# Second pair's keys and Gram matrices among the first pair's work, layernorm and evacuations on ScalarE, last products one iteration later

## The chip, the cores and the metric

The kernel runs on one core of a Trainium2 chip. A core has five engines with a queue each: TensorE (PE, matrix products; its loading of weights, PEld, overlaps them), VectorE (DVE), ScalarE (ACT), GpSimd (POOL) and SyncE (SP), which here only issues DMAs. Matrix products end in PSUM, from where DVE or ACT carries ("evacuates") them to SBUF; GpSimd doesn't touch PSUM in this kernel. Each engine runs its instructions in order and waits for the others by semaphores.

The metric is the device time of one execution in microseconds (us), as the median of several. The profile comes from one execution and has a span, from its first to its last instruction, that is a little shorter.

## What is computed

The input x has 32 sequences of 512 rows and 256 features, all in float32. A "delta rule" attention block, an MLP and a gated MLP follow, each with a layernorm ahead of it:

```python
def delta(x, ...):                       # per sequence: T = 512, C = 256
    qkv = x @ gates_w + gates_b
    q, k, v = jnp.split(qkv, 3, axis=-1)
    lr = x @ lr_w + lr_b
    k = k / jnp.linalg.norm(k, axis=-1, keepdims=True)
    K = jnp.tril(jnp.einsum('ntc,nsc->nts', k, k), k=-1)
    A = K + jnp.eye(T, dtype=x.dtype)
    u = jax.scipy.linalg.solve_triangular(A, v, lower=True)
    score = jnp.einsum('nsk,ntk->nst', q, k)
    y = jnp.einsum('nst,ntv->nsv', score, lr * u)
    return y @ out_w + out_b

x0 = x
x = norm(x);  x = x + delta(layernorm(x, dn_g, dn_b), ...)
x = x + relu(layernorm(x, mn_g, mn_b) @ w1 + b1) @ w2 + b2
x = x0 + x
h = silu(norm(x) @ wg.T) * (norm(x) @ wu.T)      # 768 hidden; int32 weights / 127
out = x + h @ wd.T
```

## The kernel before

**Tiling.** A sequence is four tiles of 128 rows (`NT`) by two halves of 128 features (`NF`). The hidden layer of the gated MLP has six tiles (`NH`). Sequences are worked on in 16 pairs (`NS` = 2). Weights of the attention block are folded into each other at the start (`Gates`, L166 to L285), so that a pair needs only keys, a Gram matrix, a triangular solve and a chain of small products.

**A pair's stages.**

1. `normalized` (L405): statistics, centring on ACT (L426), scaling on DVE (L441), two one-column copies on GpSimd; then `Turn` (L374): DVE transposes 32x32 blocks, SP writes them to DRAM and reads them back with features on the partitions (`ag`). The first pair's are transposed on PE instead (`to_features`, L365). `rates` (L460) follows. `prepare` (L850) interleaves both sequences.
2. `keys` (L476): two products of 512 columns; ACT copies `kT` and `aT`. `gram` (L491): four products of 512 to 128 columns; ACT copies the diagonal block `gd`, DVE the rest `go`. `give` (L511) sends the 32x32 diagonal blocks to DRAM.
3. `norms` (L523): the keys' norms, eight reductions on DVE and a power on GpSimd. `invert` (L543): reads the blocks of both sequences, one block's eight columns to a partition, and inverts them in 31 rows on DVE, a product (L568) and a reduction (L572) each; SP writes the result to `found` and reads it back as `yb` and into `yfull`.
4. `merge` (L595) and `solve` (L653): the blocks of 32 become blocks of 64 and 128, then the four row tiles are solved in turn (`pr`, `rhs`, `pu`, `p`, `dp`). `solution` (L861) steps both sequences.
5. `values_phase` (L939): `gather`, `through_values`, `through_keys`, `answer`: the products of the attention's output; then the layernorm for the MLP (`normed`: `Norm.measure` and `Norm.apply`, both on DVE, and a `Turn`).
6. `residual` (L767): `b2s` and `a` are added to a second load of x (`xb`), which is the running sum from then on; `mlp_in`, `mlp_out`, and a further layernorm and `Turn`.
7. Gated MLP: `gate` (L801), `up` (L815): six units each, of two products of 512 columns; `down` (L826): four units of six products of 256 columns, added to the sum, and the output.

**The order.** The order on PE, DVE and SP is the order of the program text (`manual_schedule`, L970); ACT and GpSimd are ordered by the compiler. Iteration g of the main loop (L1001) runs stages 2 to 5 of pair g (`new`), 6 and 7 of pair g-1 (`old`), and stage 1 and the keys of pair g+1 (`following`): `gram_phase`, `mlp_phase`, `gated_phase` with the gate, up and down units of the first old sequence, `solution` with the gate and up units of the second one between its steps, `values_phase`. The down units of the second old sequence wait for the next iteration's `mlp_phase` (`downs`).

Work on DVE that has no product of its own is spread by `Side` (L117): each product calls `spend` with its columns, and the side runs as many of its steps as are due by then. `INVERT` and `PREPARE` are the numbers of columns over which `invert` and `prepare` are spread:

```python
def run(self, cols):
    self.owed += cols * self.rate
    while self.owed > 0.0 and not self.over:
        w = next(self.gen, self)
```

**The start.** Before the loop, pair 0 goes through stages 1 and 2. Iteration 0 has no old pair: `gates.rest` (the rest of the weight folding), `dequant` (L291: the three int32 weights are loaded, converted on ACT, transposed on PE and copied on ACT), the inverse of pair 0, its rates and norms, then `solution` with the preparation of pair 1 as a side, and `values_phase` with the keys of pair 1. The loads of weights and biases are in part on ACT's queue (`Gates.load`, L186), ahead of its first activation.

**The end.** After the loop, `last_mlp` (L907), then gate, up and down of the last pair, one sequence after the other. The transposes of the last pair's layernorms are on PE (`turned`, L760).

## Time and profile before

| what | value |
|---|---|
| time, median of 3 runs (lowest, highest) | 2156.09 us (2153.30, 2156.43) |
| the profiled execution: time, span | 2153.22 us, 2151.4 us |
| mean clock granted to TensorE, share of full speed | 0.989 |
| bytes moved by DMA | 163.5 MB, 76 GB/s |
| share of the chain of waits: PE, DVE, ACT | 69%, 23%, 3% |
| DVE, inverse: 496 products (L568), 496 reductions (L572) | 147.2 us, 147.0 us |
| DVE, block transposes of `a`, `m` and `f` (L382) | 122.9 us |
| ACT, centring (L426): 128 activations of 128x256 | 63.2 us, 495 ns each |
| landing after issue: x again, way and `hT_m` | 6.5 us; 2.3 us and 3.7 us |

A row of a group has the line, the engine and the operation, the tiles written and read, shapes and count; then busy time and the mean of one in ns; then the engine's idle time just before these instructions and who ended it. A busy share is a mean over stages that are limited by different things. So the question is always which wait ends last in a stage, and what stands in line behind it. In tables by stage and in timelines, the first columns are start and length in us.

### The profile page before, as it was taken

The numbers are of one execution on the slowest core, as the hardware profiler recorded it, in microseconds if no ns is written. First come the engines' busy times: TensorE is split into PE (matmuls) and PEld (weight loads), VectorE is DVE, ScalarE is ACT, GpSimd is POOL, SyncE is SP. The second block draws the span as 40 slices with busy tenths as digits, with TensorE's granted clock in tenths as the row PEclk, the third lists the DMA queues.
The fourth block names the chain that finished last, engine by engine and source line by source line (L and its number), as shares of the span: only waits on it lengthen the run. The fifth ranks groups of instructions, "written<-read, shape, count | busy, mean of one in ns | idle before, by whom it ended". The sixth has DMA issues, their size and how long they took to land.

```text
span 2151.4 us, 24651 instructions
## 1 busy us (share of the span) xinstructions
PE 2062.2 (96%) x7982; PEld 1364.2 (63%) x7982; DVE 1440.2 (67%) x4570; ACT 477.3 (22%) x1179; POOL 213.0 (10%) x456
## 2 busy tenths in 40 slices
PE   5499999999999999999999999999999999999999
PEld 3365666656666675666657566675666667666665
DVE  3858585775858768585775858668585876858351
ACT  3332212222122222212222221222212222121110
POOL 2101001010100101001110100101010010100000
PEclk9599999999999999999999999999999999999999
DMA  3230232242323222332331323223232331332100
GB/s 83 62 91 18 80 99 76 72 113 61 89 64 110 82 62 79 86 94 72 88 108 52 86 76 104 76 72 92 75 86 69 106 90 52 86 83 78 37 10 20
DMA packets 233912, 163.51 MB, mean 76 GB/s; under 512 B 66485, under 2 KB 209464, under 8 KB 233784
## 3 DMA queue, kind: packets, MB, share of 16 engines
q1 hardware_dynamic: 230672, 160.23, 26.7%
q10 hardware_dynamic: 3112, 1.71, 0.4%
q8 instruction: 63, 1.03, 0.2%
q14 instruction: 65, 0.53, 0.1%
HBM read 95.82 MB, written 66.06 MB: 75 GB/s over the span
## 4 chain that ended last, share of the span: by engine, by line
PE 69%; DVE 23%; ACT 3%; issue 2%; POOL 1%; DMA 1%; ACTq 0%; DVEq 0%
PE pup L818 10%; PE pgate L806 10%; PE po_f L727 8%; PE pg L501 6%; PE pf L688 5%; PE pa L781 5%; PE po_m L727 4%; DVE xt L568 4%; PE po_d L727 4%; PE pr L667 4%; DVE xc L572 3%; PE pk L483 3%; PE pz L688 3%; PE pu L677 3%; DVE hid L823 3%; ACT a L426 2%
## 5 line engine op out<-in xcount | busy, mean ns | idle before, releaser
L818 PE MATMUL pup<-hT_f,wuT 128*128 128x512 f32 x768 | 364.0, 596 | 0.0
L806 PE MATMUL pgate<-hT_f,wgT 128*128 128x512 f32 x768 | 364.0, 596 | 0.0
L727 PE MATMUL po_f<-wdT,hid 128*128 128x256 f32 x1536 | 341.8, 379 | 3.1 <-DVE hid L823 3.1
L727 PEld LDWEIGHTS po_f<-wdT,hid 128*128 128x128 f32 x1536 | 291.0, 190 | 58.1 <-issue 12.2
L811 ACT ACTIVATE hid<-pgate 128x512 f32<-128x512 f32 x192 | 114.6, 597 | 710.5 <-PE pgate L806 705.6
L818 PEld LDWEIGHTS pup<-hT_f,wuT 128*128 128x128 f32 x768 | 143.1, 190 | 145.0 <-issue 121.0
L806 PEld LDWEIGHTS pgate<-hT_f,wgT 128*128 128x128 f32 x768 | 143.4, 190 | 138.1 <-issue 128.4
L823 DVE TENSOR_TENSOR hid<-hid,pup 128x512 f32<-128x512 f32 x192 | 131.1, 683 | 95.2 <-PE pup L818 90.7
L572 DVE TENSOR_REDUCE xc<-xt 128x8 f32<-128x16 f32 (+30 forms) x496 | 147.0, 296 | 17.0
L568 DVE TENSOR_TENSOR xt<-xc,blocks 128x16 f32<-128x16 f32 (+30 forms) x496 | 147.2, 297 | 10.4
L501 PE MATMUL pg<-kT 128*128 128x256 f32 (+3 forms) x512 | 141.4, 433 | 1.1 <-ACT kT L487 1.1
L501 PEld LDWEIGHTS pg<-kT 128*128 128x128 f32 x512 | 89.7, 190 | 60.1 <-issue 33.7
L727 PE MATMUL po_d<-m,aT 128*128 128x256 f32 x512 | 121.5, 386 | 5.1 <-DVE m L711 4.5
L727 PE MATMUL po_m<-w2s,act 128*128 128x256 f32 x512 | 119.9, 382 | 2.0
L483 PE MATMUL pk<-ag,wa 128*128 128x512 f32 x256 | 117.9, 593 | 0.4 <-ACT ag L371 0.4
L727 PEld LDWEIGHTS po_d<-m,aT 128*128 128x128 f32 x512 | 97.1, 192 | 30.8 <-DVE m L711 10.6
L781 PE MATMUL pa<-hT_m,w1s 128*128 128x512 f32 x256 | 115.3, 593 | 0.5 <-ACT hT_m L371 0.5
L688 PE MATMUL pf<-a,dp 128*128 128x256 f32 x512 | 115.7, 379 | 0.0
L727 PEld LDWEIGHTS po_m<-w2s,act 128*128 128x128 f32 x512 | 95.9, 190 | 26.8 <-ACT act L787 11.6
L680 DVE TENSOR_SCALAR dp<-pu,lr 128x256 f32<-128x256 f32 x128 | 56.7, 480 | 79.6 <-ACT p L679 67.0
L688 PEld LDWEIGHTS pf<-a,dp 128*128 128x128 f32 x512 | 97.3, 190 | 19.6 <-issue 7.2
L711 DVE TENSOR_TENSOR m<-pm,obrow 128x256 f32<-128x256 f32 x32 | 13.0, 407 | 142.2 <-ACT m L710 142.2
(159 smaller groups left out, 2483.4 us busy)
## 6 DMA issues: line engine op xcount, KB each, us to landing
x_first<-in_L_attn_x_dram SPq DMA_DIRECT2D x32, 512.0 KB, 5.6
x_again<-in_L_attn_x_dram SPq DMA_DIRECT2D x32, 512.0 KB, 6.5
out_dram<-x_again SPq DMA_DIRECT2D x32, 512.0 KB, 3.0
way_a<-turn_a SPq DMA_DIRECT2D x120, 128.0 KB, 2.4
ag<-way_a SPq DMA_DIRECT2D x30, 512.0 KB, 4.6
way_m<-turn_m SPq DMA_DIRECT2D x112, 128.0 KB, 2.3
hT_m<-way_m SPq DMA_DIRECT2D x28, 512.0 KB, 3.7
way_f<-turn_f SPq DMA_DIRECT2D x112, 128.0 KB, 2.3
```

The costliest lines, as they stand in the source:

```text
L483: nc.tensor.matmul(pk, lhsT=wa[:, f, ts(o, P)], rhs=s.ag[:, f, :], start=(f == 0), stop=(f == NF - 1),)
L501: nc.tensor.matmul(pg[:, :w], lhsT=s.kT[:, f, ts(j, P)], rhs=s.kT[:, f, j * P :], start=(f == 0), stop=(f == NF - 1),)
L568: nc.vector.tensor_tensor(t[:, :, : i + 1], xc[:, :, : i + 1], blocks[:, i, : i + 1].unsqueeze(1).to_broadcast([P, CQ, i + 1]), ALU.mult,)
L572: nc.vector.tensor_reduce(xc[:, :, i], t[:, :, : i + 1], axis=AX.X, op=ALU.add)
L667: nc.tensor.matmul(pr, lhsT=s.go[j][:, ts(i - j - 1, P)], rhs=p_[:, j, :], start=(j == 0), stop=(j == i - 1),)
L688: nc.tensor.matmul(s.pp[:, o, :], lhsT=lhs[:, c, ts(o, P)], rhs=rhs[:, c, :], start=(c == 0), stop=(c == nk - 1),)
L727: nc.tensor.matmul(self.po[:, c % 2, :], lhsT=src[:, ts(c, P)], rhs=self.w[:, f, :], start=(f == 0), stop=(f == self.nk - 1),)
L781: nc.tensor.matmul(pa, lhsT=w1s[:, f, ts(o, P)], rhs=s.hT[:, f, :], start=(f == 0), stop=(f == NF - 1),)
L806: nc.tensor.matmul(pg, lhsT=wgT[:, f, ts(o, P)], rhs=s.hT[:, f, :], start=(f == 0), stop=(f == NF - 1),)
L811: nc.scalar.activation(natural(g), grouped(pg), AF.Silu)
L818: nc.tensor.matmul(pu, lhsT=wuT[:, f, ts(o, P)], rhs=s.hT[:, f, :], start=(f == 0), stop=(f == NF - 1),)
L823: nc.vector.tensor_tensor(hid, hid, grouped(pu), ALU.mult)
```

## The change

- Start: x is loaded straight into the tile `a`, which is normalised in place and, after `residual`, is the running sum. x of both first pairs and the three int32 weights are loaded at the beginning. Pair 1 is normalised before the inverse of pair 0, transposed on PE, and its keys follow while that inverse runs. `w_down` and `w_gate` are converted after these, `w_up` between the steps of `solution`. The Gram products of pair 1 stand among the values phase of pair 0 (`first_values`).
- ACT's order is written by hand too. To ACT go the application of both inner layernorms (with `-mean * r`, a small product on GpSimd), the copy of `go` and the scaled copy `dp`. The addition of `b2s` goes to GpSimd, right after the second load of x.
- The down units of both old sequences run one iteration later, in `middle`. The gate and up units of both sequences are one stream of 24: twelve ahead of `solution`, twelve between its steps. `prepare` starts at the fourth step of `solution`.
- `invert` reads its blocks with one DMA that repeats each block for four partitions, and writes `found` with one. Its share of columns that passes before the first DVE instruction grows from 3/52 to 14/52. The unit columns come through DRAM (`Columns`).
- `through_keys` of the second sequence stands ahead of the layernorm of the first. In the last pair only the second layernorm is transposed on PE.

```diff
-    NQ = P // (NS * NB * NT)
-    CQ = B // NQ
-    PREPARE = 20 * 1024
+    PLAIN = 12
+    PREPARE = 12 * 1024
     INVERT = 22 * 1024
+    INVERT_FIRST = 14 * 1024
...
+            self.unit = const.tile([P, self.nc, B], F32, name=f"unit{n}")
...
+            nc.gpsimd.dma_start(row, first[: self.nq])
+            nc.gpsimd.dma_start(
+                self.unit, row.unsqueeze(0).to_broadcast([P // self.nq, self.nq, self.nc, B])
+            )
...
+    def load_a(s):
+        if s.a is None:
+            s.a = big(f"a_{s.n}")
+        load_x(s.n, s.a)
...
+        def turn(self, dst):
+            for r0, m, wi in self.parts:
+                wf = wi.bitcast(F32)
+                nc.scalar.mul(wf, wi, WSCALE)
+                for cc in range(self.cols // P):
+                    pt = ps_f.tile([P, 512], F32, tag="mm", name=f"{self.name}_t{cc}_{r0}")
+                    for r in range(m):
+                        nc.tensor.transpose(pt[:, ts(r, P)], wf[:, r, ts(cc, P)], ident)
+                    nc.scalar.copy(dst[:, cc, r0 * P : (r0 + m) * P], pt[:, : m * P])
+                    yield
...
+                nm = small.tile([P, NT], F32, tag="nmn", name=f"nmn_{self.tag}")
+                nc.vector.tensor_scalar(nm, self.mv[:, :, 0], -1.0, None, ALU.mult)
+                self.mr = small.tile([P, NT], F32, tag="mr", name=f"mr_{self.tag}")
+                nc.gpsimd.tensor_tensor(self.mr, nm, self.r, ALU.mult)
+
+        def apply(self, c, dst):
+            nc.scalar.activation(
+                dst, self.src[:, c, :], AF.Identity,
+                bias=self.mr[:, c : c + 1], scale=self.r[:, c : c + 1],
+            )
...
-        if n >= NS:
+        s.ag = wk.tile([P, NF, T], F32, tag="feat", name=f"ag_{n}", bufs=4)
+        if n >= 2 * NS:
...
-            nc.vector.tensor_copy(s.go[j], pg[:, P:w])
+            nc.scalar.copy(s.go[j], pg[:, P:w])
...
-        rows = P // NQ
-        for q in range(NQ):
-            nc.sync.dma_start(
-                blocks[q * rows : (q + 1) * rows], given.rearrange("s b i r c -> (s b i) r c")
-            )
+        n, nq, ncol = len(seqs), columns.nq, columns.nc
+        nc.sync.dma_start(
+            blocks,
+            given.rearrange("s b i r c -> (s b i) (r c)").unsqueeze(1).to_broadcast(
+                [n * NT * NB, nq, B * B]
+            ),
+        )
...
-        yield 3 * B
+        yield 14 * B
...
+        nc.sync.dma_start(
+            found.rearrange("s b i (q c) r -> (s b i q) (c r)", q=nq),
+            xc.rearrange("p c r -> p (c r)"),
+        )
...
-            nc.vector.tensor_scalar(s.dp[:, i, :], pu, s.lr[:, i : i + 1], None, ALU.mult)
+            nc.scalar.mul(s.dp[:, i, :], pu, s.lr[:, i : i + 1])
...
+    def by_tensor(s, stage):
+
+        return s.n < NS or (stage == "f" and s.n >= N - NS)
+
     def normed(s, stage):
 
-
-        s.h = s.norm.apply()
-        if NS <= s.n < N - NS:
-            s.turn = Turn(f"{stage}{s.n}")
+        t = Turn(f"{stage}{s.n}")
+        s.turn = t
+        if by_tensor(s, stage):
             for c in range(NT):
-                s.turn.chunk(s.h, c)
-            s.turn.send()
+                s.norm.apply(c, t.plain[:, c, :])
+            return
+        for c in range(NT):
+            h = wk.tile([P, C], F32, tag="h", name=f"h_{stage}{s.n}_{c}", bufs=3)
+            s.norm.apply(c, h)
+            t.chunk(h, c)
+        t.send()
...
+    def fetch_residual(s):
+        s.xt = wk.tile([P, NT, C], F32, tag="x", name=f"x_{s.n}")
+        load_x(s.n, s.xt)
+        nc.gpsimd.tensor_tensor(
+            s.xt, s.xt, b2s.unsqueeze(1).to_broadcast([P, NT, C]), ALU.add
+        )
 
     def residual(s):
 
-        s.acc = s.xb
-        nc.vector.tensor_tensor(
-            s.acc, s.acc, b2s.unsqueeze(1).to_broadcast([P, NT, C]), ALU.add
-        )
-        nc.vector.tensor_tensor(s.acc, s.acc, s.a, ALU.add)
+        s.acc = s.a
+        nc.vector.tensor_tensor(s.acc, s.acc, s.xt, ALU.add)
...
+    def middle(old, older, following):
+
+        one, two = old
+        rest = downs(older) if older else iter(())
+        more = lambda k: [next(rest, None) for _ in range(k)]
+        mlp_in(one, 0)
+        mlp_in(one, 1)
+        more(1)
+        mlp_out(one, 0)
+        mlp_out(one, 1)
+        mlp_in(two, 0)
+        mlp_in(two, 1)
+        normed(one, "f")
+        more(1)
+        mlp_out(two, 0)
+        mlp_out(two, 1)
+        more(1)
+        turned(one, "f")
+        normed(two, "f")
+        if following:
+            for s in following:
+                load_a(s)
+        more(5)
...
+    def first_values(seqs, following, inverse, given):
+
+        one, two = seqs
+        for _ in normalized(following[1]):
+            pass
+        gates.rest()
+        for _ in norms(0, seqs):
+            pass
+        for _ in inverse:
+            pass
+        for s in seqs:
+            for _ in rates(s):
+                pass
+        for s in following:
+            to_keys(s)
+            for o in range(NF):
+                keys(s, o)
...
+        turns = [d.turn(dst) for d, dst in quantized]
+        for turn in turns[:2]:
+            for _ in turn:
+                pass
+        turns = turns[2]
+        for _ in solution(seqs):
+            next(turns, None)
...
+        whole(gather(one))
+        whole(gather(two))
+        gram(following[0], 0)
+        whole(through_values(one))
+        gram(following[0], 1)
+        whole(through_values(two))
+        gram(following[0], 2)
+        whole(through_keys(one))
+        gram(following[0], 3)
+        give(following[0], given[0])
+        answer(one)
+        whole(through_keys(two))
+        normed(one, "m")
+        answer(two)
+        gram(following[1], 0)
+        turned(one, "m")
+        gram(following[1], 1)
+        normed(two, "m")
+        gram(following[1], 2)
+        gram(following[1], 3)
+        give(following[1], given[1])
...
             keys(following[0], 0)
+            whole(through_keys(two))
             normed(one, "m")
-            whole(through_keys(two))
...
+        load_a(first[0])
+        gates = Gates(gw)
+        load_a(first[1])
         gates.load_rest()
+        for s in pairs[1]:
+            load_a(s)
...
+                for _ in normalized(pairs[1][0]):
+                    pass
...
+                middle(old, older, following)
+                work = gated(old)
+                for i in range(PLAIN):
+                    next(work)
+                    if i == 5:
+                        turned(old[1], "f")
                 inv_side.finish()
-                for s in new:
-                    for _ in rates(s):
-                        pass
-                units = iter(())
-                prep = Side(prepare(following), 2 * 31, PREPARE)
-            kn_side.finish()
-            inv_side.finish()
-            for _ in solution(new):
-                u = next(units, None)
-                if u:
-                    u()
-                elif not old:
-                    spend(1024)
-            for u in units:
-                u()
-            values_phase(new, following, prep)
-            old = new
-        last_mlp(old, downs)
-        gated_phase(old, None)
-        for u in [*gated_units(old[1]), *down_units(old[1])]:
-            u()
+                kn_side.finish()
+                for i, _ in enumerate(solution(new)):
+                    next(work, None)
+                    if i == 3 and following:
+                        prep = Side(prepare(following), 2 * 31, PREPARE)
+                for _ in work:
+                    pass
+                values_phase(new, following, prep)
...
+        last_middle(old, older)
+        for i, _ in enumerate(gated(old)):
+            if i == 5:
+                turned(old[1], "f")
+        for _ in downs(old):
+            pass
```

## The prediction

> **What bounds the kernel.** I read first the page's busy row and its slices: is one engine full, and where not?
>
> ```profile
> PE 2062.2 (96%) x7982; PEld 1364.2 (63%) x7982; DVE 1440.2 (67%) x4570; ACT 477.3 (22%) x1179; POOL 213.0 (10%) x456
> PE   5499999999999999999999999999999999999999
> PEclk9599999999999999999999999999999999999999
> ```
>
> TensorE (PE) is full from the third slice (54 us each) on. No matmul is removed, so the change can only win idle PE time: 2151.4 - 2062.2 = 89 us, plus what PE runs slowly for want of clock. The table by stage says where that is (columns: span, then busy PE, PEld, DVE, ACT, POOL, granted clock, DMA share, GB/s):
>
> ```profile
> 0.00:24.00 24.00, 3.45 (x11) 2.31 (x12) 5.34 (x21) 5.50 (x14) 9.45 (x33) 1.00 0.56 137
> 55.00:92.00 37.00, 10.21 (x57) 8.23 (x58) 31.79 (x123) 10.84 (x28) 1.64 (x1) 0.55 0.28 82
> 92.00:112.00 20.00, 17.18 (x88) 13.43 (x88) 16.07 (x56) 6.78 (x24) 6.62 (x20) 0.72 0.00 1
> 178.00:206.00 28.00, 22.86 (x94) 14.94 (x92) 23.20 (x74) 7.26 (x22) 3.61 (x4) 1.00 0.13 33
> 590.00:718.00 128.00, 126.40 (x488) 83.48 (x488) 90.06 (x287) 28.07 (x70) 12.92 (x27) 1.00 0.29 83
> 2001.00:2100.00 99.00, 96.45 (x390) 65.85 (x389) 42.75 (x104) 18.42 (x39) 4.80 (x8) 0.98 0.04 13
> ```
>
> Idle PE: 20.6 us before the first x is normalised, 26.8 us while VectorE (DVE) inverts the first pair's blocks, 5.1 us at the end of iteration 1, about 1.8 us in each of the 14 iterations of 128.2 us from 206 to 2001 (25 us), 2.6 us near the end. What ends PE's waits after 200 us:
>
> ```profile
> PE pw L613 <- DVE xparts L606: 20.4, 29, 0.9
> PE po_d L727 <- DVE m L711: 4.5, 15, 1.6
> ```
>
> So in the steady state two places cost 1.4 and 0.2 us an iteration. The first, on DVE's timeline:
>
> ```profile
> 714.52 0.69 DVE L739 TENSOR_TENSOR x_again<-x_again,po_f 128x512 f32<-128x512 f32 x1 [2.21 <-PE po_f L727]
> 715.63 0.17 DVE L431 TENSOR_SCALAR left<-left 128x4 f32<-128x4 f32 x1 [0.42 <-ACT a L426]
> ...
> 716.61 0.30 DVE L606 STREAM_TRANSPOSE xparts<-yb 32x128 f32<-32x128 f32 x1
> ```
>
> The transposes that `merge` needs stand in DVE's order behind the normalisation of the following pair, which waits for ScalarE (ACT).
>
> **Part by part.** One 128x512 product with both contraction halves takes PE 1.72 us (four instructions), so a column of `spend` costs 1.68 ns.
>
> *Start-up.* The keys of pair 1 (4 x 1.72 = 6.9 us) leave the values phase of pair 0, where PE is full, for the hole of the inverse; that is 6.9 us of PE saved if PE is full again by then. Their gram products (8.6 us) take the keys' place as filler among pair 0's chain and gain nothing by themselves: they only move from iteration 1. Pair 1's transposes on PE (two of 0.87 us) fall in the hole: free. What is paid is the start of the hole. ACT now runs in written order: `kT` of sequence 0 stands behind the four centring activations of sequence 1 (28.5 to 30.5 us), +1.2 us on the first gram; `kT` of sequence 1 stands behind those of sequence 2 (2.0 us) and the `go` copies, +1.5. Before the inverse DVE gets: statistics and scaling of sequence 3 up to about 51.6; the gate weights, 4.2 (44.3 to 48.5 in the trace); eight norm reductions, 8 x 0.33 = 2.7, and the wait for GpSimd's power, about 2.0; then the preparation, 2.3, and 20.6 for the 31 rows (56.8 to 77.4 before). Sum 83.5 against 77.4. Afterwards less stands behind it: before, the norms (81.6 to 86.1) delayed the first transpose; now only `rates` (4.2) lies beside the DMA trip of `found` and `yb`. First transpose near 88 instead of 86.1. `solution` took 86.8 to 111.6 with pair 1's normalisation on DVE between its steps. About 3 us of the merge (bn_stats at 88.6 to 90.6 ahead of `wparts`; 94.9 to 96.3 ahead of `wl`) and 2 of the rows go with it; `w_up`'s two conversions (0.8 each) and four copies (0.6) on ACT return about 1. So it ends near 109: 2.6 us earlier. Bounds: 10 earlier, 6 later.
>
> Here a rule weighs in. The Trainium skill, "TensorE: Matmul & The Clock Gate", Part 1, says that PE falls to half clock after an idle window of about 3.4 us. The rows agree (0.55, then 0.72 while `solution` runs). One might hope that keys in the hole keep the clock up; by the rule not, since they and the weights are through by some 70 us and PE then idles until 88. With the clock at 1.00 the 17.18 us busy at 0.72 would be 12.4, 4.8 less. I take 0 of it.
>
> The six weight loads (2.25 MB) and two of x (1 MB) now stand at the head of SP's queue, ahead of nothing that SP needs before 35 us, but beside ACT's loads: these already keep ACT from its first activation until 16.1 us. Nearest row: all queues moved 137 GB/s at 0.56 busy in that window, so there is room. 0 to +5 us; I take 0, because x0, x1 and the key weights are issued first. The `unit` constant comes by two GpSimd DMAs: needed at 62 us, nothing.
>
> *Iteration 1.* It loses all its last products (PE time, kept for later), and the inverse is spread over 14k columns. DVE has 22.5 us of inverse and 5.4 of additions and statistics beside some 20 us of PE; PSUM's four buffers allow two units of lag (3.4 us). I put PE's idle time at 3 instead of 5.1: -2. Bounds -5 to +4.
>
> *Steady state.* Last products of both sequences (8 x 2.58 us) go into the middle, which is now 33k columns (8k of MLP, 12k of last products, 12k of gated ones; 55 us) long. The inverse waits 27% of its 22k columns and so runs from 10 to 38 us. DVE owes 22.5 us of it in these 28 us, and 10 of additions, statistics, transposes: it falls some 5 us behind, which costs PE nothing under four PSUM buffers of last products (5.2 us each). 12 us remain before `solution`; the trip to memory and back (706.7 to about 716) fits. The following pair's normalisation starts at step 3 of `solution`, behind the transposes. Ahead of these is only one `hid` product (0.68). L606 of sequence one is then ready 0.15 + 0.68 + 0.6 = 1.4 us after PE's last unit, under the 1.72 us of the next; that of sequence two at 2.7, against PE's 2.3. The wait falls from 1.43 to about 0.4. `through_keys(two)` now stands ahead of `normed(one)`: the 0.2 goes. Gain 1.2; I take 1.1 for small new waits. 14 x 1.1 = 15.4. Bounds: 1.7 gained, 2 lost.
>
> What ACT takes over, by the rows:
>
> ```profile
> L680 DVE TENSOR_SCALAR dp<-pu,lr 128x256 f32<-128x256 f32 x128 | 56.7, 480 | 79.6 <-ACT p L679 67.0 <-PE pu L677 12.6
> L508 DVE COPY go<-pg 128x384 f32<-128x384 f32 (+2 forms) x96 | 40.7, 424 | 41.9 <-ACT gd L505 41.3
> L350 DVE TENSOR_SCALAR h_m<-a,bnmv_m,r_m 128x256 f32<-128x256 f32 x128 | 44.2, 409 | 35.9 <-POOL r_m L321 35.9
> L770 DVE TENSOR_TENSOR x_again<-x_again,b2s 128x1024 f32<-128x1024 f32 x32 | 38.9, 1216 | 0.0
> ```
>
> Per iteration DVE loses 3.5 + 2.5 + 5.5 + 2.4 = 14 of 90 us; ACT gains 8 x 0.37 (`p` copy) + 6 x 0.42 + 16 x 0.49 (L426) = 13.3, to 41 of 128. None of it is PE time: DVE was late only at the place above. The danger is ACT's order. Behind `normed(two, "m")`, which waits for `r` (1.0 us on GpSimd after `ve`) and the new product `mr` (bounds: 0.2, a GpSimd copy, to 1.0, the power; I take 0.4), stand `kT` of the last keys and `gd`/`go` of the first gram. In the trace the last answer ends at 646.8; `mr` at 650.0; ACT free 651.7; `kT` 652.3, `aT` 652.9, first `gd`+`go` 653.6; PE wants that PSUM buffer at 654.5. Slack 0.9 us: no stall, even at 1.0. SP: `load_a` stands ahead of the last five products' output DMA; its buffer is long free.
>
> The second rule speaks against the change: "GPSIMD Engine Reference", 4.1 Engine selection, keeps two-input elementwise work off GpSimd as about twice as slow. The row is DVE's 1.22 us; by the rule an estimate of 2.4 each, 4.9 us an iteration on an engine busy 12.9. By either, the sum is the same while the additions end before `r_m`: x lands 6.5 us after its issue, `residual` needs it some 20 us on. If they stand ahead of `r_m`, it costs.
>
> *End.* Pair 15's m transposes go from PE to DMA (2 x 0.87 saved; eight last products, 20.7 us, lie around the trip of 8), and the waits of 1.6 + 0.5 + 0.5 us go: -4. Bounds -5, 0.
>
> **Sum.** -2.6 - 6.9 - 2 - 15.4 - 4 = -30.9 on the profiled execution's 2153.2 (span 2151.4): 2122. The median of three runs, 2156.1, is 2.9 above that execution: 2125.
>
> **Rivals.** (a) *Start-up gives nothing*: ACT's first activation and the longer DVE queue eat keys and idle time; 2156 - 19 = 2137. For: ACT's loads are late already; against: x0 and x1 come first. 17%. (b) *The steady wait only changes its name*: one DVE second in front of `pw` or `pr` replaces another, since normalisation is packed into 12k columns; 2156 - 15.5 = 2141. For: DVE has 16 us of it, 2.4 of `hid` and 5 of merge and rows in the 33 us of PE from there to the keys. 15%. (c) *Slower*: in `solution` ACT must centre eight chunks (8 x 0.49) between the `p` copies, in order, five steps to a unit of 1.72 us, each waiting for DVE's `nm`. If ACT is blocked longer than the unit that covers a `p`, PE stops at `pr`: two steps of 1.5 us, 3 an iteration, 15 x 3 = 45, 2156 - 31 + 45 = 2170. It decides from 2.1 us an iteration. Against: statistics are emitted two units ahead. 11%. (d) The change doing less than it says: it does move every step named. 2%. My forecast: 55%.
>
> **Numbers.** 2125 for the likeliest. All bounds at their best give some 2103, (b) with a late start about 2150: range 2105 to 2152. A difference under 0.2% (4.3 us) can't be told from none. Faster 0.83, same 0.06, slower 0.11.
>
> **What would show it.** Right: pk of pair 1 before 75 us; first `pf` near 109; iterations of about 127.1 us with `pw` waiting under 0.5 us; no new PE wait on ACT at `pg` or `pr`. Wrong: PE waiting for ACT in `solution` (c), a first activation after 18 us or `pf` after 113 (a), a period still at 128 (b).

## The result, and the profile after

The changed kernel takes 2119.54 us (median of 4 runs, 2118.80 to 2127.20); the kernel before took 2156.01 beside it. The ratio is 0.9841, 95% interval 0.9818 to 0.9865: faster by 36.5 us, against the 31 that the prediction took off. The profiled execution has a span of 2117.5 us, 33.9 less than before.

The page shows the same matmuls in the same busy time, and fewer idle microseconds of PE: 2117.5 - 2062.4 = 55.1 instead of 89. DVE's instructions fell from 4570 to 4122, ACT's rose from 1179 to 1659. These are lines of its first two parts:

```profile
PE 2062.4 (97%) x7982; PEld 1365.6 (64%) x7982; DVE 1257.1 (59%) x4122; ACT 666.7 (31%) x1659; POOL 307.3 (15%) x551
...
PE   5799999999999999999999999999999999999999
...
PEclk9799999999999999999999999999999999999999
```

The table by stage of the kernel after, with the columns of the prediction's (stretch, its length, busy PE, PEld, DVE, ACT and POOL, granted clock, DMA share, GB/s):

```profile
0.00:26.00 26.00, 2.22 (x7) 1.21 (x7) 5.34 (x21) 3.94 (x10) 9.39 (x32) 1.00 0.86 252
58.00:91.50 33.50, 24.51 (x98) 16.44 (x96) 28.85 (x112) 17.64 (x39) 1.64 (x1) 0.75 0.05 11
602.00:729.00 127.00, 126.57 (x492) 83.97 (x491) 79.36 (x260) 39.82 (x100) 18.78 (x33) 1.00 0.31 84
1993.00:2117.50 124.50, 119.33 (x449) 83.37 (x447) 35.43 (x85) 23.94 (x46) 5.23 (x10) 1.00 0.11 34
```

The second row is the hole of the first inverse: PE is busy for 24.5 of 33.5 us at a clock of 0.75, where before it was 10.2 of 37 at 0.55. The first row got worse: DMA engines 0.86 busy at 252 GB/s (before, in the first 24 us, 0.56 and 137), and PE has hardly begun after 26 us.

Waits of PE from 223 to 1995 us (what waited, on what, total, times, longest):

```profile
PE pw L644 <- DVE xparts L637: 5.1, 14, 0.4
```

One wait is left, 0.36 us an iteration. DVE's timeline shows why: the transposes follow the last `hid` product directly, and nothing of the following pair is ahead of them.

```profile
313.73 0.69 DVE L863 TENSOR_TENSOR hid<-hid,pup 128x512 f32<-128x512 f32 x1 [2.74 <-PE pup L854]
314.33 0.29 DVE L636 STREAM_TRANSPOSE xparts<-yb 32x128 f32<-32x128 f32 x1
314.64 0.30 DVE L637 STREAM_TRANSPOSE xparts<-yb 32x128 f32<-32x128 f32 x1
```

The first product of `gather` (`pf`) marks each pair. It cuts both profiled executions into the terms of the prediction's sum:

| stretch | before, us | after, us | difference | of which |
|---|---|---|---|---|
| start to the first `pf` | 111.58 | 112.84 | +1.3 | |
| to the second | 125.98 | 109.30 | -16.7 | keys -6.9, four down units moved on -10.35, rest +0.6 |
| 14 periods | 1793.5 (128.1 each) | 1770.9 (126.5 each) | -22.7 | 1.62 each |
| from the last `pf` to the end | 120.3 | 124.5 | +4.2 | four down units arrive +10.35, rest -6.1 |

The periods of the two kernels repeat to 0.2 us (the last one aside), but the start doesn't. The kernel after and three kernels of the experiments are the same up to the first `pf` (the first, third and fourth experiment change later stages only), and their traces have it at 112.84, 115.39, 113.38 and 114.16 us. So the +1.3 comes from the earliest of the four, and differences of 2 to 3 us at the first `pf` can be chance. For before there is one trace.

### The profile page after: what moved, and what is told of

It reads as the page before. It is cut to its first block, busy times and chain, and to the rows that moved or that the text cites. A ratio compares the mean times of both kernels' runs of the same rounds, so it can differ in the third digit from the quotient of the medians.

```text
span 2117.5 us, 24970 instructions
## 1 busy us (share of the span) xinstructions
PE 2062.4 (97%) x7982; PEld 1365.6 (64%) x7982; DVE 1257.1 (59%) x4122; ACT 666.7 (31%) x1659; POOL 307.3 (15%) x551
## 4 chain that ended last, share of the span: by engine, by line
PE 83%; DVE 10%; ACT 4%; issue 1%; DMA 1%; POOL 0%; ACTq 0%; DVEq 0%; SPq 0%
PE po_f L758 16%; PE pup L854 13%; PE pgate L854 11%; PE pg L533 6%; PE po_d L758 5%; PE pf L719 5%; PE pa L824 5%; PE po_m L758 5%; PE pk L515 5%; PE pm L719 3%; PE pz L719 3%; ACT a L454 2%; PE pr L698 2%; DVE bnst_a L339 2%; PE pu L708 2%
## 5 line engine op out<-in xcount | busy, mean ns | idle before, releaser
L861 ACT ACTIVATE hid<-pgate 128x512 f32<-128x512 f32 x192 | 114.3, 596 | 620.8 <-PE pgate L854 620.8
L854 PEld LDWEIGHTS pup<-hT_f,wuT 128*128 128x128 f32 x768 | 143.4, 190 | 145.8 <-issue 129.9
L758 PE MATMUL po_d<-m,aT 128*128 128x256 f32 x512 | 116.1, 380 | 1.1 <-ACT m L741 1.0
L830 ACT ACTIVATE act<-pa,b1s 128x256 f32<-128x256 f32 x128 | 53.8, 471 | 157.0 <-PE pa L824 157.0
```

Of the source, the lines that this page charges most:

```text
L758: nc.tensor.matmul(self.po[:, c % 2, :], lhsT=src[:, ts(c, P)], rhs=self.w[:, f, :], start=(f == 0), stop=(f == self.nk - 1),)
L830: nc.scalar.activation(natural(s.act[:, o, :])[:, :, some], grouped(pa)[:, :, some], AF.Relu, bias=b1s[:, o : o + 1], scale=1.0,)
L854: nc.tensor.matmul(pp, lhsT=w[:, f, ts(o, P)], rhs=s.hT[:, f, :], start=(f == 0), stop=(f == NF - 1),)
L861: nc.scalar.activation(natural(g), grouped(pp), AF.Silu)
```

## The experiments

Two questions were open. Did the steady state win by taking the normalisation out of the transposes' way, and which of the other moves does it need? And why did the start lose 1.3 us where 2.6 were to be won? Every kernel is the one after with one edit, or with several where it is said. The kernel before ran beside each group of experiments, and its medians lie between 2153.3 and 2156.2 us; so differences of 3 us between medians of different groups tell nothing, and small effects in the steady state are read from the `pf` marks of the traces.

### Preparing the following pair before `solution`

```diff
                 for i in range(PLAIN):
                     next(work)
...
+                    if i == PLAIN - 5 and following:
+                        inv_side.finish()
+                        kn_side.finish()
+                        prep = Side(prepare(following), 2 * 31, PREPARE)
...
-                for i, _ in enumerate(solution(new)):
+                for _ in solution(new):
                     next(work, None)
-                    if i == 3 and following:
-                        prep = Side(prepare(following), 2 * 31, PREPARE)
```

> The changed kernel, with the normalisation of the following pair started four gated units ahead of solution again (as in the kernel before) instead of at its fourth step. Theory (the steady gain is the place of the normalisation on DVE): the transposes of merge stand behind it again, PE waits some 1.4 us for them instead of 0.36, the period goes from 126.5 to about 127.5, the span from 2117.5 to 2131 to 2134. Rival (the gain is ScalarE's relief of DVE): span within 3 us of 2117.5.

Measured: 2208.5 us, ratio 1.025 (1.0234 to 1.0266), slower than either theory said. The period is 132.1 us in the mean of 14, 5.6 more; iteration 1 loses another 9.0. The timeline of this kernel:

```profile
327.74 0.17 DVE L459 TENSOR_SCALAR left<-left 128x4 f32<-128x4 f32 x1 [3.17 <-ACT a L454]
...
328.11 0.58 ACT L861 ACTIVATE hid<-pgate 128x512 f32<-128x512 f32 x1
...
329.41 0.68 DVE L863 TENSOR_TENSOR hid<-hid,pup 128x512 f32<-128x512 f32 x1
330.01 0.29 DVE L636 STREAM_TRANSPOSE xparts<-yb 32x128 f32<-32x128 f32 x1
...
330.76 2.31 PE L644 MATMUL pw<-xparts,gs 128*64 128x64 f32 x16 [3.91 <-DVE xparts L637]
```

The mechanism is the theory's: DVE waits 3.17 us for a centring activation, `hid` and the transposes stand behind it, and PE waits 3.91 us. (The edit also finishes the inverse before the preparation begins. That isn't the cause: `found` is issued at 316.45 us, and the transposes begin at 330.01.) Two things make it larger. ACT's order is now written out, so the SiLU that `hid` needs (L861) also stands behind the centring. And the clock falls with it: in the period from 366.1 to 498.9 us PE is busy 128.76 us at a clock of 0.97, against 126.07 at 1.00 in a period of the kernel after. So of the 6.3 us that this period is longer, some 3.6 are idle time and 2.7 slower products. The steady state's gain needs the preparation in its new place. How much of it this place wins by itself the experiment can't say, because the old place costs more here than it did before the change.

### What ACT and GpSimd took over, back on DVE

```diff
-            nc.scalar.activation(
-                dst, self.src[:, c, :], AF.Identity,
-                bias=self.mr[:, c : c + 1], scale=self.r[:, c : c + 1],
-            )
+            nc.vector.tensor_scalar(
+                dst, self.src[:, c, :], self.mv[:, c, 0:1], self.r[:, c : c + 1],
+                ALU.subtract, ALU.mult,
+            )
...
-            nc.scalar.copy(s.go[j], pg[:, P:w])
+            nc.vector.tensor_copy(s.go[j], pg[:, P:w])
...
-            nc.scalar.mul(s.dp[:, i, :], pu, s.lr[:, i : i + 1])
+            nc.vector.tensor_scalar(s.dp[:, i, :], pu, s.lr[:, i : i + 1], None, ALU.mult)
```

The addition of `b2s` goes back to DVE with them.

> The changed kernel, with the application of the layernorms, the go copy, the dp copy and the b2s addition back on DVE; the order is kept. Theory (their cost was hidden, DVE is late only ahead of merge): period 126.5 to 126.9, span 2117 to 2124, with DVE near 93 us an iteration instead of 79. Rival (the relief of DVE is the gain): period 128 or more, span 2138 or more.

Measured: 2131.41 us, ratio 0.9903 (0.9885 to 0.9920), between the two. The period is 126.6 us, 0.14 more than that of the kernel after: in the steady state the takeover is worth next to nothing, 2 us over 14 periods. The loss lies ahead of it. The first `pf` is at 120.4 us, the second 118.1 later instead of 109.3. Waits of PE between these two:

```profile
PE tp_f L391 <- DVE turn_f L372: 3.9, 1, 3.9
PE pw L640 <- DVE xparts L633: 2.4, 1, 2.4
```

Iteration 1 is short of PE work, with no down units to fill it, and has a whole inverse on DVE. There DVE is what limits, and the takeover pays. The first `pf` is 7.6 us later than in the kernel after, and 5.1 later than the latest of the four traces above. ACT's first activation came 2.7 us later here (its table load at 22.18 against 19.50 us), which this edit doesn't touch, and the profiled execution (2137.62 us) was 6.2 above the median. What the takeover is worth before the first `pf` stays open.

### The layernorm of the first sequence ahead of the second's `through_keys`

```diff
-            whole(through_keys(two))
             normed(one, "m")
+            whole(through_keys(two))
             keys(following[0], 1)
```

> The changed kernel, with the layernorm of the first sequence ahead of through_keys of the second, as in the kernel before, but now in ScalarE's written order. Theory (ScalarE's order counts, not its load): the copy of m of the second sequence stands behind four activations that wait for r; PE waits for m some 1.3 us in each of 15 iterations, span about 2137 (2130 to 2142). Rival (ScalarE at 31% has room): span 2117 to 2121.

Measured: 2131.73 us, ratio 0.9900 (0.9882 to 0.9918). The spans are 2127.4 to 2130.4 us, at the small end of the theory, and the wait is smaller than it said. Waits of PE after 223 us show this row beside the known one of `pw`:

```profile
PE po_d L758 <- ACT m L741: 4.7, 15, 0.5
```

That is 0.3 us an iteration, while the period grew by 0.67, to 127.16. Over 14 periods this is 9.4 of the 12 us. The direction is shown; the other 0.37 us are busy time of PE (126.45 us a period against 126.08), whose cause stays open.

### Last products in their own iteration

```diff
                 for _ in work:
                     pass
+                for _ in downs(old):
+                    pass
                 values_phase(new, following, prep)
```

`middle` and `last_middle` then run without down units, and `INVERT_FIRST` columns serve for all iterations.

> The changed kernel, with the last products of both sequences after the gated ones of the same iteration, ahead of the values phase, instead of one iteration later; the inverse spread over 14k columns throughout. Theory (last products are what covers the MLP's layernorm, its trip through DRAM and the inverse): the gated products wait for hT_f, 5 to 8 us an iteration, span 2190 to 2240. Rival (the same products in another order, PE full anyway): span within 6 us of 2117.5.

Measured: 2301.34 us, ratio 1.0687 (1.0670 to 1.0703), slower than the theory's 2190 to 2240. The longest row of PE's waits after 245 us:

```profile
PE pgate L854 <- DMA hT_f<-way_f: 122.6, 14, 9.1
```

Without the down units PE has nothing to do while the second layernorm goes through memory: 8.8 us an iteration. The period is 138.6 us, 12 more than after. In one of them PE is busy 129.05 us at a clock of 0.96, so 9.1 of the 12 are idle time and 3.0 slower products. Before the change one sequence's down units lay there; the new order with the units of one sequence alone was not run.

### Keys of pair 1 behind the first solution

```diff
         for s in following:
             to_keys(s)
-            for o in range(NF):
-                keys(s, o)
...
         whole = lambda gen: [None for _ in gen]
+        for s in following:
+            for o in range(NF):
+                keys(s, o)
         whole(gather(one))
```

> Pair 1's keys (transposes stay where they are) are issued after pair 0's solution instead of in the hole during the inverse. Theory (in the hole they cost nothing, later they take PE time at full clock): the keys' 6.9 us come back on the path, total 2126 to 2127, the start-up's end earlier by nothing. Rival (in the hole PE work delays the inverse's products of pair 0, or the hole's work only warmed the clock): total 2117 to 2121.

Measured: 2130.22 us (2126.10 to 2137.30). The first `pf` comes at 123.5 us, 8.1 to 10.7 later than in the four traces with the start of the kernel after. This holds the keys' 6.9; the rest is no more than those traces differ among themselves, and the table load came late here as well (21.55 us). In PE's waits of the hole, the emptied place is seen:

```profile
PE pw L644 <- DVE xparts L637: 9.9, 1, 9.9
```

In the kernel after this wait is 1.4 us. The keys fill time in which PE is otherwise idle.

### What delays the first activation

There are three edits of the start. First, the weights' loads are issued late:

```diff
-        for d, _ in quantized:
-            d.load()
...
             give(s, given[i])
+            if not i:
+                for d, _ in quantized:
+                    d.load()
```

> The six loads of the quantised FFN weights are issued after pair 0's first product is given to the inverse, instead of ahead of it. Theory (these transfers fill the DMA engines in the first 26 us, 252 GB/s against 137 in the trace of before, so ACT's issues of DMAs stall and its first activation comes at 20.8 us instead of 17.4): the first activation is back at 17 to 18 us, the first gather of pair 0 2.5 to 3.5 us earlier (about 110), total about 2116 to 2117. Rival (ACT's queue is as slow with fewer transfers, or the end of the start-up is set by the inverse and the norms of pair 1 on DVE whatever the first activation does): first gather at 112 to 113, total 2119 to 2120.

Second, the loads of pair 1's x are moved to the same place as well:

```diff
-        for s in pairs[1]:
-            load_a(s)
...
+                for n in pairs[1]:
+                    load_a(n)
```

> The loads of pair 1's x and of the quantised FFN weights are both issued after pair 0's first product is given to the inverse; ACT keeps its own DMA issues. A measurement of one thing, when the first activation starts; the total is of no interest, since pair 1's normalisation then waits for its x. Theory (the added transfers of the first 26 us, x of pair 1 above all, make ACT's DMA issues slower): the table load is back at 16 to 16.5 us, as before the change, against 19.5 after it and 18.0 with the weights alone moved. Rival (ACT's issues take this long because of what is on ACT's own queue): the table load at 18 to 19.5 us.

Third, the loads stay early, but ACT issues only those of the first cut of the gates:

```diff
-                nc.scalar.dma_start(
+                queue.dma_start(
...
-        b1s = by_feature(b1, "b1s", nc.scalar)
+        b1s = by_feature(b1, "b1s", nc.sync)
...
-        nc.scalar.dma_start(b2s, b2.partition_broadcast(P))
+        nc.sync.dma_start(b2s, b2.partition_broadcast(P))
```

> The loads for the second and third cut of the gates, the output weights and the small vectors are issued by SP's queue in place of ACT's. Theory (the first activation stands in order behind ACT's own DMA issues, while the mean it needs is there at 8.2 us): the first activation at 9 to 11 us, and the whole start-up about 9 to 10 us shorter if nothing else binds: first gather of pair 0 near 103, total about 2110. Rival (the start-up is set by another chain: loads of the gates' or weights' tensors that now land later): first gather at 109 to 113, total 2116 to 2120.

ACT's first instruction of its own is the load of its table (`ACT_TABLE_LOAD`). Its start in the trace of each kernel, with the rate of all queues in the first 26 us:

| kernel | table load, us | GB/s | first `pf`, us | median, us |
|---|---|---|---|---|
| before | 16.08 | 126 | 111.58 | 2156.01 |
| weights and x of pair 1 late | 16.74 | 132 | 119.96 | 2126.87 |
| weights late | 17.97 | 172 | 111.98 | 2122.13 |
| after | 19.50 | 252 | 112.84 | 2119.54 |
| loads on SP | 5.65 | 241 | 101.58 | 2108.87 |

These are single traces, and the table load varies from one to the next. Six further kernels of these experiments issue the same loads as the kernel after ahead of it, and with that kernel's 19.50 the seven traces have it at 18.16, 19.50, 20.11, 20.27, 20.33, 21.55 and 22.18 us. It doesn't follow the rate: the earliest had 253 GB/s and the latest 215. The kernel of the next experiment, with the weights late too, had it at 18.17.

On the timeline of the kernel after, ACT's own DMA issues (ACTq) end just before it; two of them, at L212, take 3.87 us here, and 1.30 to 3.55 in the other six. The mean that the first activation needs (`nm`) is there at 8.16 us:

```profile
7.99 0.17 DVE L449 TENSOR_SCALAR nm<-bnmv_a 128x4 f32<-128x4 f32 x1
...
8.50 3.87 ACTq L212 DMA_DIRECT2D gw<-in_L_attn_lr_w_dram  x2
...
19.12 0.35 ACTq L1091 DMA_DIRECT2D b2s<-in_L_attn_b_dram  x1
19.50 1.28 ACT L454 ACT_TABLE_LOAD   x1 [19.50 <-DMA wd_i<-in_L_ffn_w_down_dram]
```

With the loads on SP, the first activation starts as soon as that mean is there:

```profile
5.65 1.28 ACT L454 ACT_TABLE_LOAD   x1 [5.65 <-DMA a<-in_L_attn_x_dram]
8.34 0.51 ACT L454 ACTIVATE a<-a,nm 128x256 f32<-128x256 f32 x1 [1.41 <-DVE nm L449]
```

Two things follow. What costs most is shown: the first activation stands in order behind ACT's issues. With only the first cut of the gates issued there it comes 12.5 us earlier (8.34 instead of 20.80), of which 11.3 reach the first `pf` (101.58 instead of 112.84). That the loads on the other queue make ACT's issues slower is shown in direction only: with both loads late, the table load at 16.74 us is earlier than in all seven traces, near what the theory said, and about where it was before the change. How much of it belongs to the weights stays open, since 17.97 and 18.17 without them lie at the edge of what varies with them.

With the weights alone moved, the first `pf` (111.98, and 112.52 in the next kernel) is a little ahead of the four traces with them (112.84 to 115.39), but the total didn't fall; the next experiment shows why. In the kernel with both loads late, pair 1's normalisation waits for its x (DVE 9.9 us for `a`), which is why its first `pf` is late.

### A collision of DVE and GpSimd in the last iteration

In the kernel with the weights late, the last period between `pf` marks took 129.9 us, where the others take 126.5 and the same one in the kernel after 126.2. Its timeline there:

```profile
1958.50 0.30 DVE L637 STREAM_TRANSPOSE xparts<-yb 32x128 f32<-32x128 f32 x1
...
1959.08 4.69 POOL L809 TENSOR_TENSOR x<-x,b2s 128x1024 f32<-128x1024 f32 x2 [32.06 <-DMA x<-in_L_attn_x_dram]
...
1959.15 2.42 DVE L640 TENSOR_SCALAR rhs<-a,kn 128x256 f32<-128x256 f32 x1
1961.49 0.29 DVE L636 STREAM_TRANSPOSE xparts<-yb 32x128 f32<-32x128 f32 x1
...
1962.24 0.65 PE L644 MATMUL pw<-xparts,gs 128*64 128x64 f32 x8 [2.44 <-DVE xparts L637]
1962.44 1.48 DVE L640 TENSOR_SCALAR rhs<-a,kn 128x256 f32<-128x256 f32 x1
```

L640 takes 0.35 us elsewhere. Here the first ends at 1961.57, when the first of the two additions (2.35 us each) is over, and the second at 1963.92, when the other is. The transposes between them keep their 0.3 us.

In the next kernel, with the weights late as well, only the last pair's additions go to DVE:

```diff
-        nc.gpsimd.tensor_tensor(
-            s.xt, s.xt, b2s.unsqueeze(1).to_broadcast([P, NT, C]), ALU.add
-        )
+        if s.n < N - NS:
+            nc.gpsimd.tensor_tensor(
+                s.xt, s.xt, b2s.unsqueeze(1).to_broadcast([P, NT, C]), ALU.add
+            )
...
         s.acc = s.a
+        if s.n >= N - NS:
+            nc.vector.tensor_tensor(
+                s.xt, s.xt, b2s.unsqueeze(1).to_broadcast([P, NT, C]), ALU.add
+            )
```

> The kernel with the FFN weights loaded late, and in it the bias b2s of the last pair alone is added by DVE in the residual, where every other pair keeps POOL's add. With the weights late, the last period between gathers was 3.6 us longer than the others: a DVE TENSOR_SCALAR of the last inverse took 2.42 us in place of 0.35, from 0.07 us after POOL began an add of 2.35 us until that add ended. Theory (that DVE operation waits for POOL's): the TENSOR_SCALAR is back at 0.35 us, the last gather of a pair at 1992 instead of 1995.9 us, total 2118 to 2120 (the adds cost DVE up to 2 us at the end). Rival (the long operation has another cause, such as the loads then in flight): the last gather stays at 1995 to 1996, total 2121 to 2124.

Measured: 2118.84 us (2117.88 to 2119.31); all 32 instructions of that line take 352 to 355 ns, the last period is 126.2 us again instead of 129.9, and the last `pf` is at 1992.68 instead of 1995.86. The theory holds. In the kernel after, one L640 is stretched to 1.49 us in the same place, but its transposes are through by then and PE doesn't wait.

### DVE's order before the first inverse, and the sum of the start's edits

The remaining gates and the norms are put between the steps of pair 1's second normalisation, and the rates between those of `solution`:

```diff
-        for _ in normalized(following[1]):
-            pass
+        gen, gn = normalized(following[1]), norms(0, seqs)
+        for _ in range(9):
+            next(gen)
         gates.rest()
...
-            for _ in rates(s):
-                pass
...
         for _ in solution(seqs):
             next(turns, None)
+            for r in rs:
+                next(r, None)
+                next(r, None)
```

> In the start-up the folding of the remaining gates is put between the statistics and the scaling of pair 1's second sequence, the key norms among it, and the learning rates' steps into the solution. Theory (DVE sets the start-up between 48 and 89 us and idles 4.1 us waiting for an activation and about 2 us for the key norms): inverse some 4 us earlier, first gather at 107.5 to 109, total about 2114 to 2116. Rival (the inverse's own chain between PE and DVE sets the end, and work pushed beside it slows it as much): first gather within 1 us of 112.8, total 2119 to 2121.

Measured: 2119.11 us, no difference in the time. The inverse is done earlier: SP issues `found` at 82.10 us instead of 85.23. PE's first `pw` in the kernel after, and in this one:

```profile
90.30 2.34 PE L644 MATMUL pw<-xparts,gs 128*64 128x64 f32 x16 [1.39 <-DVE xparts L637]
```

```profile
87.17 2.34 PE L644 MATMUL pw<-xparts,gs 128*64 128x64 f32 x16 [3.78 <-DVE xparts L637]
```

So 3.1 us are won here, but the first `pf` is only 0.7 earlier (112.14). From `pw` to `pf` it takes 25.0 us instead of 22.5: the rates are now among the steps, and PE's clock in this stretch is 0.67 instead of 0.77. The clock's part may be chance: in the three other traces with the start of the kernel after, the stretch takes 23.2 to 23.7 us at a clock of 0.66 to 0.69.

With the loads on SP as well:

> Both of the earlier start-up edits in one kernel: the loads for the later cuts of the gates, the output weights and the small vectors are issued by SP, and the remaining gates are folded between the statistics and the scaling of pair 1's second sequence. Theory (the two cuts lie in different stretches of one chain, before 20 us and from 48 to 89 us, so they add): the 11 us of the first and the 0.7 to 1.5 us of the second, first gather near 100.5, total about 2107 to 2108. Rival (with the loads on SP the gates' remaining weights land later, and the fold in its new place waits for them): first gather at 102 or later, total 2109 to 2112.

Measured: 2106.69 us (2105.22 to 2108.98), ratio 0.9773 (0.9759 to 0.9786), first `pf` at 98.49: 14.4 us before that of the kernel after, 3.1 before the loads on SP alone. This pair is the cleaner comparison, because both have a clock of 0.67 from `pw` to `pf`. There the order on DVE wins 4.3 us at `pw` (73.57 instead of 77.85) and loses 1.2 of them again up to `pf` (24.9 instead of 23.7 us). The times themselves, 2106.69 and 2108.87, are too near to each other to tell. The weights late on top of that:

> As the kernel with both start-up edits, and the quantised FFN weights are also issued after pair 0's first product is given to the inverse. Theory (with ACT free of DMA issues nothing in the first 26 us waits for the DMA engines any more, so moving these transfers gives nothing): within 1 us of the kernel with both edits, about 2107 to 2109. Rival (the loads on SP still stand behind these transfers): another 1 to 3 us less, 2104 to 2106.

Measured: 2106.68 us, first `pf` at 99.66. There is no further gain, as the theory had it. The kernel with both edits, or with the loads on SP alone (2108.87, 0.9774 to 0.9801), beats the changed one (0.9818 to 0.9865) by 11 to 13 us.

## Why the prediction was right, and which terms were not

The direction and the mechanism held, and the time, 2119.5 against 2125, lies in the range. By the steps of the sum:

- **Steady state** (predicted -15.4, measured -22.7). The wait at `pw` fell from 1.4 to 0.36 us and the one behind `m` went, as predicted, for the reason predicted: nothing of the following pair stands ahead of the transposes, and the first experiment shows that the wait returns, and longer, when it does. The term was too small: I took 1.1 of the 1.2 reckoned, "for small new waits", and none came; the measured idle time fell by 1.34 and PE's busy time, which I held fixed, by another 0.27.
- **Keys in the hole** (-6.9). Moving them out again cost 8.1 to 10.7 us at the first `pf`, so the bet that PE is full again by then held.
- **Start** (predicted -2.6, measured +1.3). The step that failed is "0 to +5 us; I take 0, because x0, x1 and the key weights are issued first". That they are issued first doesn't help, because what is late is ACT's issue of its own loads: the first activation came 3.4 us later than before, where 0 was taken. 137 GB/s at 0.56 busy was read as room; with these loads added, the table load came at 18.16 to 22.18 us in seven traces, against 16.08 before. Behind it, the queue on DVE up to `merge` was reckoned 1.8 us too long (first transpose predicted near 88, measured 89.6 with the 3.4 in it), and the solution 2.2 too short (21 us predicted, 23.2 measured from there to `pf`): together 3.8 (3.4 - 1.8 + 2.2), the first `pf` at 112.84 instead of 109. With a start that varies by 2 to 3 us, the split is that of this trace. The sign named for rival (a), a first activation after 18 us, appeared at 20.8, but the rival as a whole (2137) didn't: its keys were won.
- **Iteration 1** (predicted -2, measured +0.6). PE's idle time between the two `pf` marks fell from 5.45 to 4.22 us, less than I put, and its busy time fell by 15.45 instead of the 17.25 of the keys and down units that left; why these products ran 1.8 us longer stays open. The experiment with the work back on DVE shows that this iteration is where DVE limits.
- **End** (predicted -4, measured -6.1). Waits and transposes went as reckoned. Left out was that `po_d`, behind the wait of 1.6 us, had also run at 449 ns each instead of 383: 32 of them are 2 us.
- **ACT's order** (rival c, and the slack of 0.9 us at `gram`). No PE wait on ACT is left in the steady state. In the solution ACT's copies of `p` do stand behind six centring activations (330.96 to 333.92 us in the trace), and PE has other products to run. The Trainium skill's rule about GpSimd ("GPSIMD Engine Reference", 4.1 Engine selection) gave the length of the additions (estimate 2.4, measured 2.35 us). They end before `r_m` (at 362.3 us, where `r_m` starts at 366.1), so they cost nothing in the steady state.
- **The loads of the engines.** DVE's busy time in a period fell by 11.3 us (90.2 to 78.9) where 14 were reckoned, and ACT's rose by 11.8 (28.1 to 39.8) where 13.3 were. Neither moved PE.
- **Rival (b)**, a wait that changes its name: one wait remains, under its old name, a quarter as long.

The clock has to be told by itself. The forecast that the keys would not keep it up held, but not for the reason given. PE did not idle from 70 to 88 us: the transposes of the weights, which wait for ACT's conversions, go on to 88.9, and from 76 us to the first `pw` no wait of PE is longer than 1.4 us. The clock fell in their midst (columns as in the table by stage):

```profile
76.00:80.00 4.00, 1.84 (x10) 1.12 (x10) 3.62 (x12) 3.08 (x11) 0.00 (x0) 1.00 0.00 0
80.00:82.00 2.00, 0.77 (x3) 0.41 (x3) 1.86 (x5) 1.87 (x6) 0.00 (x0) 0.53 0.00 0
84.00:90.30 6.30, 2.28 (x10) 1.43 (x9) 5.91 (x27) 3.40 (x6) 0.00 (x0) 0.50 0.24 49
```

So the fall did not take an idle window of 3.4 us, the figure quoted in the prediction: in this trace PE was busy for 46% of the four microseconds ahead of it.

On the profiled executions the terms measured are +1.3 - 6.9 + 0.6 - 22.7 - 6.1 = -33.8, against -30.9 predicted. I put the gain of the steady state and of the end 9.4 us too small, and that of the start and of iteration 1 6.5 us too large. That the total came so near is in part luck.

## What to carry to other kernels

When a wait sits behind work that another stage put in the engine's order, ask where that work could stand instead, and check in the new place what is queued behind each of its waits: the same `prepare` eight units earlier cost 89 us. At a kernel's start, look for an engine that both issues loads and computes; here its issues alone held the first activation 12.5 us, and giving them to a queue that computes nothing won more than any other edit of the start. A stage that gets faster hands its gain to the next one only as far as that one is ready for it: 4.3 us won at `pw` became 3.1 at `pf`, because work moved out of the first stage went into the second. And before a difference of 2 us in a start-up is explained, see how far traces of the same start lie apart.

## What the runs showed of the hardware

A DVE TENSOR_SCALAR of 128x256 in float32 that starts 0.07 us after a GpSimd addition of 128x1024 takes 2.42 us instead of 0.35 and ends within 0.2 us of the addition's end; the block transposes of 32x128 beside the second addition keep their 0.3 us. The Trainium skill, "SBUF — State Buffer", section "SBUF: two separate sides", describes this: some DVE operations and all of GpSimd's take one pair of ports in turn, each for a whole instruction. The runs agree, and they add how much hangs on a little: in the kernel after, the addition begins 0.18 us behind the first L640 of the last inverse and costs nothing; where it began 0.07 us ahead of it, the iteration took 3.7 us more.

DMA issues on ACT end later when more loads go out on SP's queue at the same time, although the two are different queues: ACT's table load behind them started at 16.08 us in the kernel before and at 16.74 with the loads of the weights and of pair 1's x moved away, and at 18.16 to 22.18 in seven traces with these loads. The spread of 4 us among those seven is as large as the effect. The Trainium skill, "DMA: Bandwidth & Descriptors", section "Issuing engines are not separate DMA queues", says that the DMAs of all issuing engines run on the same 16 DMA engines, which would fit, though no run here shows that this is the reason; and that the time it takes to initiate a DMA is usually small beside the DMA itself. Here the time for 22 of them added up: it held ACT until 19.5 us.
